# Self-attention rows of groups two to four: read turned from memory and normalised in place, instead of normalised and turned with TensorE

## The chip, the cores and the metric

The kernel runs on one core of one Trainium2 chip. The metric is the device time of one execution in microseconds (us). A core has five instruction streams that run side by side and wait for one another: TensorE (PE; its weight loads are listed apart as PEld), VectorE (DVE), ScalarE (ACT), GpSimd (POOL) and SyncE (SP, which issues most DMAs; POOL and ACT issue a few).

## The reference

The program is one decoder layer in float32 on 16 sequences of 128 rows, 1024 wide. Only its first stage matters here, single-head self-attention on the layer-normalised rows, per sequence of 128 rows, with a head of width 256:

```
x = x + attn(layernorm(x))
def layernorm(x): m = mean(x); v = var(x); return (x - m) / sqrt(v + 1e-5)
def attn(x):
    q, k, v = split(x @ Wqkv + bqkv, 3)            # Wqkv is 1024 x 768
    a = softmax(q @ k.T / sqrt(256))               # per sequence
    return (a @ v) @ Wo + bo                       # Wo is 256 x 1024
```

Cross-attention with a context and a feed-forward block with packed 4-bit weights follow. They make up the rest of the time and are not touched by the change.

## The kernel before

**Layout.** The 16 sequences are the residual tiles X[0] to X[15] (128 x 1024 each, 512 KB). Self-attention works in four groups t = 0..3 of four sequences. For each group it needs the normalised rows turned, a tile xnT of 128 x 8 x 512: eight chunks of 128 input columns, each over the 512 rows of the group.

**How xnT is made.** For a sequence b, `row_stats` (L130, L131) takes mean and variance on DVE; `row_rstd` (L135, L136) makes 1/sqrt(var + eps), an addition on DVE and a power on POOL; `normalise` (L139) writes xn on DVE; `turn_half` (L344) turns xn with four TensorE transposes into a PSUM tile `tr`, twice per sequence; and `turn` copies the two halves into xnT, one on DVE (L351) and one on ACT (L352). The first group has a version of its own, `first_rows`, with the normalisation on ACT (L152) and the copies on L63 and L368; its DVE instructions go through the wrapper InOrder (L63), which keeps them in program order among themselves.

**A group's work.** `query_key` (L397) multiplies the q and k columns of Wqkv with xnT, four blocks f of eight matmuls, copied out by ACT (L406). `value` (L412) makes v for each of the four sequences, with the bias added on DVE (L419). `weigh` (L427) makes the scores; DVE takes the row maximum (L435, L436), ACT the exponential (L440), DVE the reciprocal and the product `at` (L448, L449). `turn_weights` turns `at` (L457, copied by DVE, L459) and `attend` (L467) multiplies with v; ACT copies the result oT (L470). In the next group, between the blocks f, `give` (L295) multiplies oT with Wo and DVE adds it to X (L302). `add_bias` (L390) adds the output bias to X[b] on POOL, one 128 x 1024 addition per sequence; it needs the tile bo_sb. During group t the rows of group t+1 are normalised and turned.

**Beside it.** `early` is a generator that unpacks the feed-forward's 4-bit weights on DVE in the same stage: tiles pa and pc on L63, loads raw and sz on SP (L197, L198), stores on POOL (L214). Its steps are drawn between the blocks of groups 1 to 3.

**What orders the work.** Each engine runs its list of instructions strictly in its order. The lists are laid out when the program is built, by a scheduler that knows the dependences and estimates durations, not by the order of the source alone; the instructions of InOrder keep their own order, and others are put between them. DMAs of SP use eight completion counters in turn, so an SP DMA is not issued before the eighth one ahead of it has landed. The loads of the start are issued by SP in this order: X[0..3] (L329), five pieces of Wqkv (L332), the bias of v (L333), X[4..7] (L335), Wo (L336, 1 MB), bo_sb (L337, 512 KB), X[8..15] (L339), then the first raw and sz.

Of the kernel before, what the change touches and what calls it, by code (L numbers as in the profile page):

```python
# [11 lines left out]
F32 = mybir.dt.float32  # L12
I32 = mybir.dt.int32
AF = mybir.ActivationFunctionType
ALU = mybir.AluOpType
# [3 lines left out]
P = 128  # L19
B, S, C = 16, 128, 1024  # L20
# [5 lines left out]
EPS = 1e-5  # L26
CC = C // P
NB = C // P
TB = 512
BPT = TB // S  # L30
NT = B // BPT
JC = C // 2 // P
HB = B // 2
Q = 32
# [32 lines left out]
def decoder_layer(  # L67
    ctx: ExitStack,
    tc: tile.TileContext,
    x: bass.AP,  # L70
    cx: bass.AP,
    cxt: bass.AP,
    wqkv: bass.AP,
# [22 lines left out]
    nc = tc.nc  # L96
# [3 lines left out]
    small = ctx.enter_context(tc.tile_pool(name="small", bufs=4))  # L100
# [8 lines left out]
    X = []  # L109
# [12 lines left out]
    mv = stat.tile([P, B, 2], F32, name="mv")  # L122
    rstd = stat.tile([P, B], F32, name="rstd")
    mhalf = const.tile([P, BPT], F32, name="mhalf")
    nc.vector.memset(mhalf, -0.5)

    def row_stats(b, vector=nc.vector):
        st = small.tile([P, 2, 6], F32, name="bnst")
        for h in range(2):
            vector.bn_stats(st[:, h, :], X[b][:, ts(h, 512)])  # L130
        vector.bn_aggr(mv[:, b, :], st)  # L131

    def row_rstd(b0, n, vector=nc.vector):
        r = rstd[:, ds(b0, n)]
        vector.tensor_scalar(r, mv[:, ds(b0, n), 1], EPS, None, ALU.add)  # L135
        nc.gpsimd.tensor_tensor(r, r, mhalf[:, :n], ALU.pow)  # L136

    def normalise(dst, src, b):
        nc.vector.tensor_scalar(  # L139
            dst, src, mv[:, b, 0:1], rstd[:, b : b + 1], ALU.subtract, ALU.mult  # L140
        )
# [27 lines left out]
    dram = ctx.enter_context(tc.tile_pool(name="wdram", bufs=1, space=bass.MemoryType.DRAM))  # L169
# [145 lines left out]
    with (  # L315
# [17 lines left out]
        nc.sync.dma_start(bv_sb, bv.partition_broadcast(P).rearrange("p o f -> p (o f)"))  # L333
        for b in range(BPT, 2 * BPT):
            nc.sync.dma_start(X[b], x[b])  # L335
        nc.sync.dma_start(wo_sb, wo.rearrange("(dc p) c -> p dc c", p=P))  # L336
        nc.sync.dma_start(bo_sb, bo.partition_broadcast(P).rearrange("p o f -> p (o f)"))  # L337
        for b in range(2 * BPT, B):
# [2 lines left out]
        def turn_half(xn, xnT, b, h):  # L341
            tr = atr.tile([P, 4, P], F32, name="tr")
            for j in range(4):
                nc.tensor.transpose(tr[:, j, :], xn[:, ts(4 * h + j, P)], ident)  # L344
            return xnT[:, ts(h, 4), ts(b % BPT, S)], tr

        def turn(b, xnT):

            xn = a2.tile([P, C], F32, name="xn")
            normalise(xn, X[b], b)  # L350
            nc.vector.tensor_copy(*turn_half(xn, xnT, b, 0))  # L351
            nc.scalar.copy(*turn_half(xn, xnT, b, 1))  # L352

        def first_rows(xnT):

            vector = InOrder(tc, nc.vector)
            halves = {}

            def stats(b):
                row_stats(b, vector)  # L360
                row_rstd(b, 1, vector)

            def rows(b):
                xn = a2.tile([P, C], F32, name="xn")
                row_shift(b, vector)
                normalise_act(xn, X[b], b)
                halves[b] = turn_half(xn, xnT, b, 0)
                nc.scalar.copy(*turn_half(xn, xnT, b, 1))  # L368

            def copy(b):  # L370
                vector.tensor_copy(*halves[b])

            for fn, b in (
                (stats, 0),
                (stats, 1),
                (rows, 0),
                (rows, 1),
                (stats, 2),
                (copy, 0),
                (copy, 1),  # L380
                (stats, 3),
                (rows, 2),
                (rows, 3),
                (copy, 2),
                (copy, 3),
            ):
                fn(b)

        def add_bias(b):
            nc.gpsimd.tensor_tensor(X[b], X[b], bo_sb, ALU.add)  # L390

        def query_key(f, xnT, qkT, ps=None, tokens=slice(None)):

            if ps is None:
                ps = aps.tile([P, TB], F32, name="mm")
            for c in range(CC):
                nc.tensor.matmul(  # L397
                    ps[:, tokens],
                    wqkv_sb[:, f, c, :],
                    xnT[:, c, tokens],  # L400
                    start=(c == 0),
                    stop=(c == CC - 1),
                )
            if tokens == ts(0, TB // 2):
                return
            nc.scalar.activation(qkT[:, f, :], ps, AF.Identity, bias=bqk_sb[:, f : f + 1])  # L406

        def value(i, xnT, v):

            ps = aps.tile([P, DH], F32, name="mm")  # L410
            for c in range(CC):
                nc.tensor.matmul(  # L412
                    ps,
                    xnT[:, c, ts(i, S)],
                    wqkv_sb[:, 4:6, c, :],
                    start=(c == 0),
                    stop=(c == CC - 1),
                )
            nc.vector.tensor_tensor(v[:, i, :], ps, bv_sb, ALU.add)  # L419
# [34 lines left out]
        def turn_weights(at):  # L454
            tr = atr.tile([P, BPT, S], F32, name="tr")
            for i in range(BPT):
                nc.tensor.transpose(tr[:, i, :], at[:, i, :], ident)  # L457
            atT = a1.tile([P, BPT, S], F32, name="atT")
            nc.vector.tensor_copy(atT, tr)  # L459
            return atT  # L460

        def attend(atT, v):
            oT = ag.tile([P, 2, TB], F32, name="oT")
            for d in range(2):
                ps = aps.tile([P, BPT, S], F32, name="mm")
                for i in range(BPT):
                    nc.tensor.matmul(  # L467
                        ps[:, i, :], v[:, i, ts(d, P)], atT[:, i, :], start=True, stop=True
                    )
                nc.scalar.copy(oT[:, d, :], ps.rearrange("p i s -> p (i s)"))  # L470
            return oT

        def give(b, oT):
            for h in range(2):
                give_half(b, h, oT, [wo_sb[:, d] for d in range(2)], aps)

        xnTs = [a2.tile([P, CC, TB], F32, name="xnT")]
        first_rows(xnTs[0])  # L480
        oT = None
        for t in range(NT):
            xnT = xnTs.pop()
            more = t + 1 < NT
            if more:
                xnTs.append(a2.tile([P, CC, TB], F32, name="xnT"))
                for b in range((t + 1) * BPT, (t + 2) * BPT):
                    row_stats(b)
                row_rstd((t + 1) * BPT, BPT)
            qkT = a2.tile([P, 4, TB], F32, name="qkT")  # L490
            halves = {}
            if t == 0:

                for f in range(4):
                    halves[f] = aps.tile([P, TB], F32, name="mm")
                    query_key(f, xnT, qkT, halves[f], ts(0, TB // 2))
            for f in range(4):
                if t == 0:
                    query_key(f, xnT, qkT, halves[f], ts(1, TB // 2))
                else:  # L500
                    query_key(f, xnT, qkT)
                add_bias(t * BPT + f)
                if more:
                    if oT is not None:
                        give((t - 1) * BPT + f, oT)
                    turn((t + 1) * BPT + f, xnTs[0])
                if t > 0:
                    for _ in range(1 + f % 2):
                        next(early, None)
            v = a2.tile([P, BPT, DH], F32, name="v")  # L510
            value(0, xnT, v)
            at = weigh(qkT)
            if more:
                value(1, xnT, v)
                value(2, xnT, v)
                atT = turn_weights(at)
                value(3, xnT, v)
                if t == 0:
                    for _ in range(3):
                        next(early)  # L520
            else:

                for i in range(1, BPT):
                    give((t - 1) * BPT + i - 1, oT)
                    value(i, xnT, v)
                    next(early, None)
                atT = turn_weights(at)
                give(t * BPT - 1, oT)
            oT = attend(atT, v)
            for _ in range((3, 3, 3, 0)[t]):  # L530
                next(early, None)
# [106 lines left out]
    if True:  # L638
# [163 lines left out]
        def query_unit(b, pair, qs, wait):  # L802
# [43 lines left out]

            later(2, weigh)
            later(wait, turn)

        def turned(b):  # L850
# [800 lines left out]
    with ExitStack() as dst:  # L1651
# [126 lines left out]
        for n, oq in enumerate(DOWN):  # L1778
# [23 lines left out]
            for iq in INNER:  # L1802
# [13 lines left out]
                if iq == 1:  # L1816
                    t = kept["u"] = dt.tile(wide, F32, name="iu")
# [3 lines left out]
                elif iq == 6:  # L1821
                    t = kept["u"]
# [90 lines left out]
```

## Time and profile before

| what | value |
|---|---|
| device time, median of 3 runs | 2226.76 us (2226.05 to 2232.44) |
| span of the profiled execution | 2228.8 us |
| busy share of PE, DVE, ACT, POOL | 98%, 70%, 23%, 25% |
| self-attention stage | about 0 to 250 us |
| first matmul of `attend` in groups 0, 1, 2, 3 | 62.83, 125.85, 189.64, 248.78 us |
| first transposes on PE | 9.33 us |

The page gives the span of the profiled execution and no other time of it; the span lies inside the three runs. The page's first part says how long each engine was busy; the chain of waits follows the work that ended last back from the end, so that time on it is time of the kernel; the timeline lists instructions with their start and duration, and in brackets the idle time of the engine before them with what ended it. A matmul in float32 shows as two records. Spans of matmuls include a latency that overlaps with the next one, so the cost of a run of matmuls is read from start to start, or from the chain.

### The profile page before, as it was taken

To read this page: it belongs to the slowest core of one execution; us is meant where nothing else is said; L and a number is where in the kernel's file an instruction comes from. 1 tells how busy PE (TensorE), PEld (TensorE's weight loads), DVE (VectorE), ACT (ScalarE), POOL (GpSimd) and SP (SyncE) were. 2 spreads that over 40 slices of the span, in tenths; PEclk is the share of its full clock that TensorE was granted. 3 is DMA by queue.
4 is the path that set the end of the run, shared out by engine and by line. 5 is a ranking of instruction groups with operands and counts; after the bars stand their busy time and mean duration, and the time that the engine had idled before them with its cause. 6 is when DMAs were issued, how large, how long until landed. Compare 5 with 4: busy or idle time off the path is not lost.

```text
span 2228.8 us, 24449 instructions
## 1 busy us (share of the span) xinstructions
PE 2192.9 (98%) x8500; PEld 1547.7 (69%) x8500; DVE 1563.4 (70%) x2119; ACT 508.5 (23%) x684; POOL 564.2 (25%) x442
## 2 busy tenths in 40 slices
PE   8999999999999999999999899999999999999998
PEld 7556555555555544444888488888887788888887
DVE  7897577888887637667799778787786645544462
ACT  2111235665556531111121112122121000000000
POOL 5453133333333300001354134444442000000000
PEclk9999999999999999999999999999999999999999
DMA  6435447777796748899544835465555965334631
GB/s 253 158 130 185 142 144 242 226 228 231 234 290 190 241 137 263 254 292 303 183 135 137 231 113 164 158 199 164 167 195 180 346 200 179 101 124 138 219 118 40
DMA packets 268725, 425.27 MB, mean 191 GB/s; under 512 B 28784, under 2 KB 130544, under 8 KB 268464
## 3 DMA queue, kind: packets, MB, share of 16 engines
q1 hardware_dynamic: 239584, 368.54, 52.7%
q0 software_dynamic: 10704, 35.92, 4.4%
q10 hardware_dynamic: 18304, 19.14, 2.7%
q8 instruction: 70, 1.15, 0.2%
q14 instruction: 63, 0.52, 0.1%
HBM read 265.62 MB, written 157.35 MB: 190 GB/s over the span
## 4 chain that ended last, share of the span: by engine, by line
PE 88%; DVE 6%; DMA 3%; issue 2%; SPq 1%; ACT 0%; POOL 0%; DVEq 0%; ACTq 0%; POOLq 0%
PE q L63 24%; PE po L1792 21%; PE p L63 11%; PE kq L63 10%; PE mm L63 8%; PE kx L63 5%; PE mm L397 4%; PE p L1166 2%; DVE pa L63 2%; PE mm L412 2%; PE mm L295 1%; DVE ti L63 1%; DMA wd<-pc 1%; PE tr L344 1%; DVE C L63 1%
## 5 line engine op out<-in xcount | busy, mean ns | idle before, releaser
L63 PE MATMUL q<-ti,li 128*128 128x256 f32 x1176 | 271.6, 380 | 2.9 <-DVE ti L63 1.4
L63 PEld LDWEIGHTS q<-ti,li 128*128 128x128 f32 x1176 | 222.5, 190 | 37.0 <-POOL li L63 4.5
L63 POOL TENSOR_TENSOR li<-w 128x512 f32<-128x512 f32 x98 | 141.2, 1443 | 342.9 <-DMA wd<-pc 235.2
L63 PE MATMUL p<-b,w 128*128 128x512 f32 x432 | 194.1, 602 | 12.5 <-DVE h L63 12.0
L825 POOL TENSOR_TENSOR qe<-qe,qrec 128x1024 f32<-128x1024 f32 x64 | 148.1, 2314 | 180.1 <-DVE qrec L63 156.0
L63 ACT COPY k<-q 128x512 f32<-128x512 f32 x147 | 86.0, 585 | 468.8 <-PE q L63 467.6
L1792 PE MATMUL po<-wc,lc 128*128 128x256 f32 x840 | 183.4, 379 | 0.0
L1792 PEld LDWEIGHTS po<-wc,lc 128*128 128x128 f32 x840 | 159.6, 190 | 21.8
L63 PEld LDWEIGHTS p<-b,w 128*128 128x128 f32 x432 | 82.9, 193 | 118.0 <-issue 100.9
L63 PE MATMUL p<-T,w 128*128 128x512 f32 x304 | 134.7, 592 | 0.0
L1792 PE MATMUL po<-wq,lq 128*128 128x256 f32 x560 | 126.7, 379 | 0.3 <-issue 0.3
L63 PEld LDWEIGHTS mm<-qs,m_sb 128*128 128x128 f32 x512 | 97.3, 190 | 40.1 <-issue 29.4
L63 DVE STREAM_TRANSPOSE kt<-qe 128x1024 f32<-128x1024 f32 x64 | 79.4, 1240 | 64.5 <-POOL qe L825 58.1
L63 PE MATMUL kq<-wq_sb,xn 128*128 128x512 f32 x256 | 120.3, 593 | 1.6 <-ACT qe L813 1.6
L63 PE MATMUL kx<-ek,cxt 128*128 128x512 f32 x256 | 121.8, 598 | 0.0
L63 PE MATMUL mm<-qs,m_sb 128*128 128x256 f32 x512 | 120.8, 379 | 0.0
L63 PE MATMUL kq<-wk_sb,cx 128*128 128x512 f32 x256 | 120.1, 592 | 0.0
L1792 PEld LDWEIGHTS po<-wq,lq 128*128 128x128 f32 x560 | 106.0, 190 | 15.9 <-issue 1.1
L397 PE MATMUL mm<-xnT,wqkv_sb 128*128 128x512 f32 (+1 forms) x320 | 113.2, 510 | 0.0
L63 POOL TENSOR_TENSOR li<-w,li 128x512 f32<-128x512 f32 x49 | 66.3, 1352 | 183.7 <-PE q L63 172.6
L63 DVE TENSOR_TENSOR pa<-pa,sz 128x1024 f32<-128x1024 int32 x86 | 108.8, 1265 | 2.4
L63 PEld LDWEIGHTS p<-T,w 128*128 128x128 f32 x304 | 57.8, 190 | 72.7 <-issue 72.2
(193 smaller groups left out, 3759.9 us busy)
## 6 DMA issues: line engine op xcount, KB each, us to landing
w<-wu SPq DMA_DIRECT2D x140, 256.0 KB, 3.5
lq<-h SPq DMA_DIRECT2D x140, 256.0 KB, 4.4
w<-wg SPq DMA_DIRECT2D x138, 256.0 KB, 2.9
kd<-kt SPq DMA_DIRECT2D x64, 512.0 KB, 3.7
qs<-kd SPq DMA_DIRECT2D x256, 128.0 KB, 3.5
h<-hc SPq DMA_DIRECT2D x80, 256.0 KB, 2.9
wq<-wd SPq DMA_DIRECT2D x70, 256.0 KB, 5.2
h<-h SPq DMA_DIRECT2D x60, 256.0 KB, 2.1
```

Source lines behind the costliest of these rows:

```text
L63: return lambda *args, **kw: self._tc.keep_in_program_order(fn(*args, **kw))
L295: tensor.matmul(ps, oT[:, d, ts(b % BPT, S)], wo_d[d][:, ts(h, 512)], start=(d == 0), stop=(d == 1),)
L344: nc.tensor.transpose(tr[:, j, :], xn[:, ts(4 * h + j, P)], ident)
L397: nc.tensor.matmul(ps[:, tokens], wqkv_sb[:, f, c, :], xnT[:, c, tokens], start=(c == 0), stop=(c == CC - 1),)
L412: nc.tensor.matmul(ps, xnT[:, c, ts(i, S)], wqkv_sb[:, 4:6, c, :], start=(c == 0), stop=(c == CC - 1),)
L825: nc.gpsimd.tensor_tensor(qe, qe, rec.unsqueeze(2).to_broadcast(wide), ALU.mult)
L1166: tensor.matmul(ps, wt[:, j, :], T[q][:, :, j], start=(first == q and j == 0), stop=(q in (2, 3, 4) and j == JC - 1), skip_group_check=True,)
L1792: nc.tensor.matmul(bank[:, i, :], l[:, ts(i, S)], w,  start=(start and c == 0 and i % 2 == 0), stop=(stop and c == len(pairs) - 1), skip_g ...
```

## The change

For groups 1 to 3 the transposes on PE, the tile xn and the copies out of PSUM are gone. The host hands over a second copy of the input, `xt`, in the layout of xnT; `load_rows` loads it with two DMAs of 1 MB per group straight into the xnT tile. Now the rows lie along the free dimension, and the mean and the scale of a row have to be the same in all partitions. `spread_stats` makes them so: after the statistics, an addition on DVE, a power on POOL and a multiply on DVE put rstd and -mean*rstd of the group's four sequences into eight columns of a tile gst; DVE turns gst in 32 x 32 blocks; four DMAs of 8 x 32 elements write it into a DRAM tile; one DMA reads that back, spread over all partitions, as `both` (128 x 2 x 512, 512 KB). `normalise_part` then works on xnT in place on DVE, two chunks at a time: a product with the first half of `both` and a sum with the second, two tensor-tensor instructions of 128 x 1024, four times per group. The per-group `row_rstd` goes. The load of group 1 stands between X[4..7] and Wo among the loads of the start; those of groups 2 and 3 are issued when the xnT tile two groups back is free. `first_rows` is as before.

```diff
@@ loads of the start
         for b in range(BPT, 2 * BPT):
             nc.sync.dma_start(X[b], x[b])
+        xnTs = [a2.tile([P, CC, TB], F32, name="xnT") for _ in range(2)]
+        def load_rows(t):
+            for h in range(2):
+                nc.sync.dma_start(xnTs[-1][:, ts(h, CC // 2)], xt[t, :, ts(h, CC // 2)])
+        load_rows(1)
         nc.sync.dma_start(wo_sb, wo.rearrange("(dc p) c -> p dc c", p=P))
         nc.sync.dma_start(bo_sb, bo.partition_broadcast(P).rearrange("p o f -> p (o f)"))
@@ helpers
-        def turn(b, xnT):
-            xn = a2.tile([P, C], F32, name="xn")
-            normalise(xn, X[b], b)
-            nc.vector.tensor_copy(*turn_half(xn, xnT, b, 0))
-            nc.scalar.copy(*turn_half(xn, xnT, b, 1))
+        gst = aw.tile([P, Q], F32, name="gst")
+        nc.gpsimd.memset(gst, 0.0)
+        def spread_stats(t):
+            r, sh = (gst[:, ds(8 * t + 4 * n, BPT)] for n in range(2))
+            m = mv[:, ds(t * BPT, BPT)]
+            nc.vector.tensor_scalar(r, m[:, :, 1], EPS, None, ALU.add)
+            nc.gpsimd.tensor_tensor(r, r, mhalf, ALU.pow)
+            nc.vector.scalar_tensor_tensor(sh, m[:, :, 0], -1.0, r, ALU.mult, ALU.mult)
+            rows = small.tile([P, Q], F32, name="gst_rows", bufs=2)
+            nc.vector.transpose(rows, gst)
+            flat = dram.tile([8, 4, Q], F32, name="gst_flat", tag="gst_flat", bufs=2)
+            for q in range(4):
+                nc.sync.dma_start(flat[:, q], rows[ds(Q * q + 8 * t, 8)])
+            both = a2.tile([P, 2, TB], F32, name="both", tag="xn")
+            flat = flat.rearrange("(w i) q s -> w (i q s)", w=2)
+            nc.sync.dma_start(both, flat.partition_broadcast(P))
+            return both
+        def normalise_part(xnT, f, both):
+            part = xnT[:, ts(f, 2)]
+            for w, op in ((0, ALU.mult), (1, ALU.add)):
+                nc.vector.tensor_tensor(
+                    part, part, both[:, w].unsqueeze(1).to_broadcast([P, 2, TB]), op
+                )
@@ the loop over groups
-        xnTs = [a2.tile([P, CC, TB], F32, name="xnT")]
         first_rows(xnTs[0])
         oT = None
         for t in range(NT):
-            xnT = xnTs.pop()
+            xnT = xnTs.pop(0)
             more = t + 1 < NT
             if more:
-                xnTs.append(a2.tile([P, CC, TB], F32, name="xnT"))
+                if t > 0:
+                    xnTs.append(a2.tile([P, CC, TB], F32, name="xnT"))
+                    load_rows(t + 1)
                 for b in range((t + 1) * BPT, (t + 2) * BPT):
                     row_stats(b)
-                row_rstd((t + 1) * BPT, BPT)
+                both = spread_stats(t + 1)
...
                     if oT is not None:
                         give((t - 1) * BPT + f, oT)
-                    turn((t + 1) * BPT + f, xnTs[0])
+                    normalise_part(xnTs[0], f, both)
@@ host
+        "xt": a["x"].reshape(NT, TB, CC, P).transpose(0, 3, 2, 1),
```

More of the change, by code (lines that the diff above doesn't have):

```diff
@@ L70, in decoder_layer @@
     x: bass.AP,
+    xt: bass.AP,
     cx: bass.AP,
```

## The prediction

> **What bounds the kernel now.** I read the page's busy shares first, then the chain of waits, then the stage that the change touches, from the timelines of PE, DVE, POOL and SP between 0 and 250 us. From the page, the chain that ended last, by engine:
>
> ```profile
> PE 88%; DVE 6%; DMA 3%; issue 2%; SPq 1%; ACT 0%; POOL 0%; DVEq 0%; ACTq 0%; POOLq 0%
> ```
>
> TensorE sets the time. In the self-attention stage the list of waits has PE idle for 9.3 us at the start and 1.0 us after it (0.83 before the second group's `attend`, 0.2 before a transpose). Some pieces of the same chain, kept to this stage (start, length, what):
>
> ```profile
> 9.33 3.68 PE tr L344 x16
> ...
> 33.09 0.87 PE tr L344 x8
> ...
> 59.54 3.47 PE mm L412 x16
> 63.03 0.04 DVE v L419
> ...
> 139.19 0.87 PE tr L344 x8
> ```
>
> One sequence's eight transposes cost PE 0.87 us, 0.109 each, against twice that (0.23) for the very first ones. The chain leaves PE at 63.03 and comes back at 127.5: in the second group DVE is all but the bound. Busy time by stretch says the same (the columns are PE, PEld, DVE, ACT, POOL):
>
> ```profile
> 80.00:100.00 20.00, 20.00 (x60) 9.66 (x59) 19.90 (x29) 2.55 (x4) 13.24 (x14) 1.00 0.46 151
> 100.00:120.00 20.00, 20.00 (x86) 14.14 (x85) 19.90 (x38) 2.45 (x9) 7.56 (x12) 1.00 0.51 174
> ```
>
> DVE is busy for 19.9 us in 20 here, while PE never stops. So PE time removed is a gain only while DVE keeps pace.
>
> POOL's additions of the output bias, and the DVE products beside one of them:
>
> ```profile
> 26.47 17.78 POOL L390 TENSOR_TENSOR X<-X,bo_sb 128x1024 f32<-128x1024 f32 x7 [0.55 <-issue]
> 44.21 1.02 POOL L136 TENSOR_TENSOR rstd<-rstd,mhalf 128x4 f32<-128x4 f32 x1
> 45.20 2.36 POOL L390 TENSOR_TENSOR X<-X,bo_sb 128x1024 f32<-128x1024 f32 x1
> 85.62 3.21 POOL L390 TENSOR_TENSOR X<-X,bo_sb 128x1024 f32<-128x1024 f32 x1
> ```
> ```profile
> 79.09 1.20 DVE L63 TENSOR_TENSOR pa<-pa,sz 128x1024 f32<-128x1024 f32 x1
> ...
> 87.14 2.77 DVE L63 TENSOR_TENSOR pa<-pa,sz 128x1024 f32<-128x1024 f32 x1
> ```
>
> An addition takes 2.36 us alone and 3.2 beside a DVE product, which then takes 2.77 instead of 1.20. POOL begins at 26.47, as soon as bo_sb is there: SP issued it at 13.52 and it took 12.8 to land.
>
> **What is removed.** 96 transposes, 12 sequences at 0.87 us: 10.4 us of PE, all on the path: 3.5 in each of groups 0, 1 and 2. ACT's 12 copies were off it (ACT 23% busy). DVE loses 12 copies (0.68 us, 0.60 from start to start) and 12 normalisations (0.72 alone, up to 2.8 beside POOL).
>
> The Trainium skill's page "TensorE: Matmul & The Clock Gate", Part 4 on the PE-mode transpose, has one at about 275 ns in a kernel; this trace has 292 as a mean duration, but the eight start 0.109 us apart. By the page's figure the change would take away 26 us and win; the spacing decides, and the sum goes by 0.87.
>
> **What is added, and where it falls.** I read the lists of the changed kernel, built but not run. After self-attention they are the same on all engines, so what is lost or won by then stays. In the first group they are not. POOL (its rows 11 to 22) and DVE (rows 50 to 59):
>
> ```
> 11 L364 TensorTensor gst<-gst,mhalf 128x4            (power, group 1)
> 12-21 L420 TensorTensor X<-X,bo_sb 128x1024          (ten bias additions, X[0] to X[9])
> 22 L364 TensorTensor gst<-gst,mhalf 128x4            (power, group 2)
>
> 50 L363 TensorScalarPtr gst<-mv 128x4                (group 2)
> 51 L365 TensorScalarPtr gst<-mv,gst 128x4            [waits Pool]
> 52 L367 StreamTranspose gst_rows<-gst 128x32
> 53-58 L380 TensorTensor xnT<-xnT,both 128x1024, x8   (group 1)
> 59 L449 TensorTensor v<-mm,bv_sb 128x256             (group 0)
> 60 L465 TensorReduce nmax<-mm 128x4                  (group 0)
> ```
>
> So group 2's power stands behind ten bias additions, DVE waits for that power, and behind this wait stand all of group 1's normalisation and then group 0's own v and softmax, for which PE waits. Step by step:
>
> 1. The 2 MB of xt stand ahead of Wo and bo_sb in SP's queue. Between 18.68 and 22.53 SP issues a load every 1.28 us, each as the eighth before it lands, so 512 KB land in 1.28 us and 2 MB in 5.1. bo_sb landed at 13.52 + 12.8 = 26.3; now at 31.4.
> 2. Ten additions at 2.36: 31.5 + 23.6 = 55.1. The power, 1.02: 56.1. Two small DVE instructions (0.14 for the row `shift`; the 32-wide transpose between 0.06 and 1.24, from 1.24 for 128x1024; I take 0.2): 56.5.
> 3. Eight tensor-tensor instructions of 128x1024. In place with a spread operand they are like pa<-pa,sz: 1.20 each, 9.6. POOL goes on with X[10] and X[11] beside them; beside two earlier additions DVE lost 1.56 us in one product and 2.0 in two (4.50 for 2.48), so two cost 0 to 4, I take 3.6. DVE reaches v at 69.7 (66.1 to 72).
> 4. From v to `at` ready: before, v at 51.01 and `at` at 56.09 with a wait for PE inside; without it v, maximum and scale 1.3, ACT and the rest 2.55: 3.95 in all. Then PE's transposes of `at` (0.44) and the last `value` (3.46).
> 5. PE has nothing after its third `value`. Its first rows are late as well (DVE's list has the statistics of X[4] and X[5], which land at 18.7 and 20.0, ahead of the shifts for X[2] and X[3]), by some 5 us; it would get to the wait near 48, and it waits until about 74. That hides the 5 us, and all of group 0's saved 3.5.
> 6. After the idle start of the run PE needed 4.5 us (9.33 to about 13.9) until its spacing fell to the full rate, and lost half of it. The granted clock reads 1.00 there all the same. After 26 us of idle I take the same 2.2; the other end is 0.
>
> `attend` of group 0 then starts at 69.7 + 3.95 + 3.9 + 2.2 = 79.8, against 62.83: **17.0 late**.
>
> The same page of the Trainium skill ("TensorE: Matmul & The Clock Gate", Part 1, on the clock gate) lets PE fall to half rate after an idle window of about 3.4 us and back after as long a busy one. By that step 6 would be 1.7 instead of 2.2. It speaks against any change that trades PE work for a PE wait.
>
> **Groups 1 and 2.** From there to the second `attend` DVE took 64.0 us (63.37 to 127.38). It loses four copies (2.4), two normalisations (1.4), the wait for POOL and two more (2.8), statistics that move behind (1.5) and two bias additions beside it, now earlier (1.56 + 2.0); it gains eight products of 1.2 (9.5): 61.8, and up to 3 more for X[12] and X[13]. PE needs 64.7 - 1.0 - 3.5 = 60.2. I take 62.5, **2.2 back** (0 to 4.5). Behind DVE's two new waits (power, then `both`) stand the bias sums that free PSUM; group 1's `both` is hidden by the wait above: its last gst write is issued when X[11] lands (36.6), queued behind X[15] (37.7 + 5.1 = 42.8), and two DMAs at 4 to 5 us (2 KB of bqk took 4.0, raw 3.5) end by 52.
>
> In group 2 PE has 62.1 - 3.5 = 58.7. DVE had 50.3 busy, with 6 us lost beside POOL; it gains 9.6, loses 4.3 (copies, two normalisations), takes over 1.5 and drops about 3 of the loss: 54. Group 3's power stands behind the additions to X[12..15], and four writes and `both` follow: some 4 us of DVE wait. That just fits; I take 1 us of stall, **2.5 back** (0 to 3.5). SP's loads of xt wait for PE to leave the old xnT and hold up raw and sz behind them; each 1 MB lands in about 4.6 (2 + 2.6), before DVE asks for it 5.7 us later.
>
> **Sum.** 17.0 - 2.2 - 2.5 = 12.3. The profiled span of 2228.8 becomes 2241.1; it lies 2.0 above the median of the runs, so the time is 2226.8 + 12.3 = **2239**. With every term at its low end (v at 66.1, no slow restart: 11.1; 4.5 and 3.5 back) it is +3.1, 2230. At the high end (v at 72: 19.2; nothing back) it is +19.2, 2246; a gst chain longer than bounded may add two.
>
> **Rivals.**
> - *The hold is weak* (2233, chance 0.17): no loss beside POOL and no slow restart, as in the low end, or one of them. For it: DVE's products beside the addition at 85.62 lost nothing until 87.1. Against: the rows above.
> - *Faster* (2222, chance 0.08): group 1's normalisation starts when `both` lands, not when POOL's tenth addition is done. At 47 it would end at 56.6, `attend` would start at 64.5, 1.7 late, and 2.2 to 8 come back: -0.5 to -6.3. It decides if normalising begins before about 50. Against: DVE's list is in order and row 51 stands ahead of 53; for it, only that additions may take less time with DVE quiet, and 2.345 is the shortest of ten.
> - *DVE bound to the end* (2247, chance 0.17): additions beside it and the two chains of small DMAs eat all that groups 1 and 2 give back. For it: 19.9 in 20.
> - That the transposes stay is no case: the list of PE has only the first group's and those of `at`.
>
> **How the numbers follow.** The forecast (2234 to 2245) has 0.56, the rest as above, 0.02 for anything else. A measurement here tells 0.3%, 6.7 us, from no change: below 2220 is faster, above 2233.5 slower. Of the faster rival about half passes the bound: 0.04. Same: the rest of it and two thirds of the weak hold, 0.16. Slower: 0.80. The range 2230 to 2248 leaves out the faster rival and a tail above.
>
> **What would show it.** PE idle for 20 to 28 us before the first transposes of `at`; POOL's first bias addition near 31.5 and its second power of four near 55; DVE idle before that, then eight products in 10 to 14 us; `attend` of group 0 near 80; the last `attend` 9 to 15 later than 248.78. It is wrong if v of group 0 comes before 62, or if the third `attend` trails by under 5.

## The result, and the profile after

The changed kernel takes **2244.43 us** (median of 4 runs, 2243.06 to 2246.63); the kernel before took 2229.0 in the same setting (median of 4, 2226.05 to 2232.44). The ratio is 1.007, with a 95% interval of 1.0054 to 1.0087: slower by 15 us. The profiled execution has a span of 2241.4 (2228.8 before) and a time of 2243.25. The forecast was 2239 in a range of 2230 to 2248.

Where does it go? First the changed kernel's chain of waits by engine, as the page has it:

```profile
PE 84%; DVE 8%; DMA 4%; issue 2%; POOL 2%; ACT 1%; SPq 0%; DVEq 0%; ACTq 0%; POOLq 0%
```

PE's share of the chain fell from 88% to 84%; DVE, POOL and DMA took it over. In the list of PE's waits (what waits and for what: us in total, times, longest) two rows grew and one shrank; before they had 9.3, 0.2 and 12.0:

```profile
PE tr L353 <- ACT xn L153: 15.3, 2, 9.7
PE tr L487 <- DVE at L479: 15.1, 2, 10.1
PE p L63 <- DVE h L63: 8.7, 2, 6.5
```

The first has the known 9.7 at the start and a new 5.6; the second is PE's wait for the softmax weights, in groups 0 and 2; the third lies far behind the stage. The longer pieces of the chain itself, in order of time (start, length, what), show who made the wait of group 0:

```profile
36.56 18.55 POOL X L420 x8
55.10 0.99 POOL gst L364
56.12 4.62 DVE gst L365
60.90 9.13 DVE xnT L380 x8
70.36 0.61 DVE nmax L465
71.25 1.51 ACT at L470 x8
73.00 0.70 DVE at L479
73.84 1.09 PE tr L487 x4
74.93 5.35 PE mm L442 x16
```

These are bias additions on POOL, the power behind them, DVE's small sum (gst) that waits for the power, eight products, and only then group 0's own softmax. No PE work stands in it between 36 and 73. POOL's timeline has the additions (start, length, line, operation, in brackets the idle time before it); beside it DVE's row for the small sum:

```profile
31.93 23.17 POOL L420 TENSOR_TENSOR X<-X,bo_sb 128x1024 f32<-128x1024 f32 x10 [3.51 <-DMA bo_sb<-in_bo]
55.03 1.05 POOL L364 TENSOR_TENSOR gst<-gst,mhalf 128x4 f32<-128x4 f32 x1
56.02 4.69 POOL L420 TENSOR_TENSOR X<-X,bo_sb 128x1024 f32<-128x1024 f32 x2
```
```profile
56.12 4.61 DVE L365 SCALAR_TENSOR_TENSOR gst<-mv,gst 128x4 f32<-128x4 f32 x1 [17.13 <-POOL gst L364]
```

Read the two together. The sum over 128 x 4 elements takes 0.16 us elsewhere. Here it starts 0.10 after POOL has begun the additions to X[10] and X[11] and ends at 60.73, 0.02 after they do. By these times it did not run slowly; it was held until both additions were done. How the hold falls differs from kernel to kernel: in stats_pinned and warm, two of the experiments below, where POOL's list is the same here, the sum took 2.30 beside the first of the two additions, and the eight products 11.13 and 11.16 (9.13 here) beside the second. Together that is 4.1 to 4.2 us lost instead of 4.5. PE's side of it, and below it the same three rows of the kernel before:

```profile
73.84 1.09 PE L487 MATMUL tr<-ident,at 128*128 128x128 f32 x4 [10.07 <-DVE at L479]
74.72 5.54 PE L442 MATMUL mm<-wqkv_sb,xnT 128*128 128x256 f32 x16
80.10 2.06 PE L497 MATMUL mm<-atT,v 128*128 128x128 f32 x16
```
```profile
58.94 0.60 PE L457 MATMUL tr<-ident,at 128*128 128x128 f32 x4
59.37 3.62 PE L412 MATMUL mm<-wqkv_sb,xnT 128*128 128x256 f32 x16
62.83 2.06 PE L467 MATMUL mm<-atT,v 128*128 128x128 f32 x16
```

After a wait of 10.07 the four transposes take 1.09 instead of 0.60 and the `value` 5.54 instead of 3.62, and `attend` of group 0 starts at 80.10 instead of 62.83. The granted clock reads 0.50 from 73.84 to 78.00. This is called the slow restart below. The start of `attend` in each group is the best ruler for this stage; the interval of a group is the time from the start before to its own. For all kernels, with these starts as PE's timeline has them (those of the kernel before differ by 0.17 from the small table in groups 2 and 3) and the ratio to the kernel before on the same chip:

| kernel | attend 0 | 1 | 2 | 3 | median us (runs) | ratio, 95% interval |
|---|---|---|---|---|---|---|
| before | 62.83 | 125.85 | 189.47 | 248.61 | 2229.0 (4) | |
| changed | 80.10 | 139.35 | 206.16 | 265.30 | 2244.43 (4) | 1.0054 to 1.0087 |
| adds_moved | 68.39 | 127.65 | 194.77 | 253.91 | 2231.72 (10) | 1.0007 to 1.0026 |
| stats_pinned | 80.09 | 139.34 | 205.97 | 265.12 | 2244.5 (4) | 1.0047 to 1.0081 |
| no_norm | 60.07 | 125.82 | 184.96 | 244.10 | 2223.82 (10) | 0.9964 to 0.9983 |
| warm | 76.97 | 136.22 | 202.58 | 261.72 | 2243.55 (4) | 1.004 to 1.0074 |
| adds_late | 68.74 | 128.11 | 187.42 | 252.79 | 2235.71 (6) | 1.0021 to 1.0044 |
| late_stats | 71.41 | 130.67 | 189.95 | 255.32 | 2237.8 (6) | 1.0031 to 1.0056 |
| late_stats_bo | 74.83 | 134.08 | 193.16 | 258.51 | 2240.59 (5) | 1.004 to 1.0066 |
| before_load | 69.39 | 136.07 | 198.72 | 257.85 | 2237.7 (7) | 1.0021 to 1.0045 |
| before_load_pinned | 65.59 | 129.57 | 193.19 | 252.33 | 2232.53 (11) | 1.0013 to 1.0031 |
| dve_adds | 67.41 | 130.39 | 189.58 | 248.72 | 2226.51 (12) | 0.998 to 0.9997 |
| before_dve | 62.21 | 125.10 | 188.72 | 247.86 | 2227.97 (11) | 0.9988 to 1.0006 |
| dve_adds_act | 66.57 | 128.90 | 189.71 | 248.85 | 2225.45 (11) | 0.9983 to 1.0001 |

The last `attend` of the changed kernel is 16.7 late, the span only 12.6, while the medians of the runs differ by 15.4. In these two profiled executions 4.1 us come back later, mostly in the third row of the waits above (12.0 to 8.7). That row varies by 1 to 3 us between kernels with the same work there (8.7 to 12.0 in the runs below), so totals a few us apart say less than the `attend` columns.

### The profile page after: what moved, and what is told of

It is laid out like the page before. It is cut to its first block, busy times and chain, and to the rows that moved or that the text cites. A ratio compares the mean times of both kernels' runs of the same rounds, so it can differ in the third digit from the quotient of the medians.

```text
span 2241.4 us, 24271 instructions
## 1 busy us (share of the span) xinstructions
PE 2188.3 (98%) x8404; PEld 1542.8 (69%) x8404; DVE 1559.8 (70%) x2125; ACT 501.0 (22%) x672; POOL 558.2 (25%) x443
## 4 chain that ended last, share of the span: by engine, by line
PE 84%; DVE 8%; DMA 4%; issue 2%; POOL 2%; ACT 1%; SPq 0%; DVEq 0%; ACTq 0%; POOLq 0%
PE q L63 23%; PE po L1823 21%; PE p L63 11%; PE kq L63 10%; PE mm L63 8%; PE kx L63 5%; DVE pa L63 2%; PE p L1197 2%; DMA X<-in_x 1%; DVE ti L63 1%; POOL X L420 1%; PE mm L427 1%; PE mm L442 1%; DVE xnT L380 1%; DMA szd<-in_dsz 1%
```

## The experiments

**The theory:** the time is lost on POOL and DVE: bias additions on POOL stand ahead of the power and hold DVE, PE waits, and loses more through a slow restart. **The rivals:** the late first rows; the loads of `xt` and the late bo_sb; the normalisation's own DVE time, which would leave nothing to gain wherever the additions stand.

### adds_moved: the additions out of group 1's way

```diff
-                add_bias(t * BPT + f)
+            for b in (range(0, 8), (), range(8, 12), range(12, 16))[t]:
+                add_bias(b)
```

The loop stands behind spread_stats(t + 1), with add_bias on POOL through InOrder.

> The bias additions are placed by hand on POOL: X[0] to X[7] ahead of group 2's power, X[8..11] in group 2, X[12..15] in group 3. Theory (the hold on POOL and DVE makes the loss): the second power moves from 55.0 to about 50.6 and no addition runs beside the small DVE sum behind it (4.6 us becomes 0.2), so the eight products run from 52 to 61, the first attend starts near 69.4 instead of 80.1, and the stall of group 2 shrinks because X[12..15] are no longer added at its start: 10 to 16 us less than the changed kernel. Rival (DVE simply has too much work, the hold is a symptom): the first attend comes earlier, but groups 1 and 2 stretch and at most 5 us are won.

Measured: 2231.72, 12.7 us under the changed kernel. The power of group 2 ran at 50.12 instead of 55.03, nothing stood beside DVE's small sum (0.16), PE waited 1.71 and restarted at full rate: 4.9 + 4.5 + 2.4 make the 11.7 by which `attend` 0 came earlier. The rows of adds_moved:

```profile
50.12 1.04 POOL L364 TENSOR_TENSOR gst<-gst,mhalf 128x4 f32<-128x4 f32 x1
51.20 0.16 DVE L365 SCALAR_TENSOR_TENSOR gst<-mv,gst 128x4 f32<-128x4 f32 x1 [10.23 <-POOL gst L364]
64.47 0.63 PE L487 MATMUL tr<-ident,at 128*128 128x128 f32 x4 [1.71 <-DVE at L479]
```

That part is settled. The power still stands behind eight additions, and `attend` 0 is still 5.6 later than before; no run puts the power ahead of all additions while they stay on POOL. The expected shrinking of group 2's stall failed: PE waited 5.90 there (4.98 in the changed kernel). The reason is in the timelines of adds_moved, DVE and POOL in group 2:

```profile
136.98 2.31 DVE L365 SCALAR_TENSOR_TENSOR gst<-mv,gst 128x4 f32<-128x4 f32 x1 [0.94 <-POOL gst L364]
139.21 2.91 DVE L63 TENSOR_TENSOR pc<-pa 128x512 f32<-128x512 f32 x1
142.03 0.20 DVE L367 STREAM_TRANSPOSE gst_rows<-gst 128x32 f32<-128x32 f32 x1
142.16 5.18 DVE L63 TENSOR_TENSOR pc<-pc,pa 128x512 f32<-128x512 f32 x1
```
```profile
136.92 4.64 POOL L63 TENSOR_TENSOR X<-X,bo_sb 128x1024 f32<-128x1024 f32 x2
141.51 0.60 POOL L215 DMA_DIRECT2D wg<-pa  x1
142.14 4.65 POOL L63 TENSOR_TENSOR X<-X,bo_sb 128x1024 f32<-128x1024 f32 x2
```

The additions to X[8..11], which the edit put into group 2, now do there what others did in group 0: sums that take 0.16, 0.68 and 0.68 took 2.31, 2.91 and 5.18, 8.9 us more.

### stats_pinned: the first rows on time

```diff
-                    row_stats(b)
+                    row_stats(b, InOrder(tc, nc.vector) if t == 0 else nc.vector)
```

> The statistics of X[4..7] are kept behind the first rows' DVE instructions. Theory: PE's wait of 5.6 us ahead of the transposes of X[2] and X[3] goes, PE then waits longer before the transposes of the weights, the first attend stays within 1 us of 80.1 and the time within 2 us of the changed kernel. Rival (the late start is paid for once more): 5 to 7 us less.

Measured: 2244.5, and `attend` 0 at 80.09 (80.10). PE's wait for the third xn is 1.29 instead of 5.64, and its wait for the weights 17.99 instead of 10.07. The late first rows cost nothing here; that rival is out.

### no_norm: without statistics and products

```diff
-                for b in range((t + 1) * BPT, (t + 2) * BPT):
-                    row_stats(b)
-                both = spread_stats(t + 1)
...
-                    normalise_part(xnTs[0], f, both)
+                    pass
```

> Leaves out, for groups 1 to 3, the statistics, the spreading and the products, so q, k and v of these rows come from x as it was loaded. Theory (96 transposes are worth 10.4 us of PE, the loads of xt cost nothing by themselves): all DVE waits of PE in self-attention go and the time is 10 to 12 us below the kernel before. Rival (the loads, or something beside the transposes, cost as well): less than 6 us below it.

Measured: 2223.82, 5.2 us faster than before, not 10 to 12. Group 0 gains 2.8, but group 1 has a PE wait of 4.03 for `at` and a slow restart (1.09, 5.59). POOL's sixteen additions follow one another there from 32.52 to 72.30, and four DVE instructions beside them, between 60.95 and 72.58, take 2.0 to 2.2 us more each than alone, 8.4 together; that is more than the wait. So half of the 10.4 us of transposes does not come back here even when the normalisation is free, and POOL's additions are the likely cause; no run takes them out of no_norm.

### warm: PE kept busy through its wait

```diff
+                if t == 0:
+                    spare = atr.tile([P, 4, P], F32, name="tr")
+                    for n in range(22):
+                        tc.keep_in_program_order(
+                            nc.tensor.matmul(spare[:, 0:2].rearrange("p a b -> p (a b)"),
+                                xnT[:, n % CC, ts(0, S)], wqkv_sb[:, 4:6, n % CC, :], start=True, stop=True))
                 atT = turn_weights(at)
```

> 22 products of 128x256 into a spare PSUM tile (9.5 us, results unused) fill PE's wait in group 0. Theory (an idle PE starts again at half rate): from the transposes of the weights to the first attend it takes 3.9 to 4.2 us instead of 6.3, the first attend starts 2.2 us earlier and the time is about 2 us less. Rival (the slow stretch comes from the engines around it): no change in either.

Measured: with PE busy until 0.32 before the transposes these took 0.63, the `value` 3.62, and `attend` 0 started 3.92 after the transposes instead of 6.26. The restart is worth 2.3 us, and idle time makes it. In the stage it is won: the last `attend` starts 3.6 earlier. The total moved by 0.9 (2243.55), inside the spread; group 2's wait (4.93, with its slow restart) was still there.

### adds_late and late_stats: no addition in groups 1 and 2

Against adds_moved:

```diff
-            for b in (range(0, 8), (), range(8, 12), range(12, 16))[t]:
+            for b in (range(0, 8), (), (), range(8, 16))[t]:
```

> As adds_moved, but the bias additions to X[8] to X[15] all stand in group 3, where DVE has no products; none is left in groups 1 and 2. Theory A: in adds_moved group 2 stalled because four additions at 136.92 to 146.79 on POOL held DVE (the 128x4 sum took 2.31 instead of 0.16, two 128x512 sums 2.91 and 5.18 instead of 0.68: 8.9 us together), so the PE wait of 5.90 for the weights of group 2 and the slow restart behind it go: interval of group 2 from 67.1 to about 59.2, last attend at 246 to 248 (253.91 in adds_moved), total 2224 to 2227. Rival B: DVE is simply full in group 2, products included, and the stall of at least 4 us stays wherever the additions are: last attend 251 to 254, total 2230 to 2233. Rival C: the eight additions in group 3 hold DVE there, and the stall moves to group 3: intervals 59, then 65 or more.

Measured: the stall of group 2 is gone (no wait, interval 59.31), as theory A had it; rival B is out. DVE still waits 2.94 for `both` in that group (2.67 in the changed kernel), so that wait alone does not stall PE. Rival C is right too: in group 3 the interval grew to 65.4. DVE's and POOL's rows of adds_late there:

```profile
199.24 14.35 DVE L63 TENSOR_TENSOR pc<-pc,pa 128x512 f32<-128x512 f32 x1
213.51 0.68 DVE L63 TENSOR_TENSOR pc<-pa 128x512 f32<-128x512 f32 x1
```
```profile
199.19 13.84 POOL L63 TENSOR_TENSOR X<-X,bo_sb 128x1024 f32<-128x1024 f32 x6
```

One sum of 128 x 512 elements, 0.68 us of work, stood for 14.35 us: as long as six additions that follow one another without a gap. It is the clearest line of this study, and late_stats and late_stats_bo repeat it: the same sum takes 14.33 in both. (Not every sum waits for a whole run: just before it, sums of 1.22 and 0.68 took 3.25 and 2.73, one addition each.) The last `attend` (252.79) and the total missed theory A. The total was 2235.71, 4 above adds_moved, though the stage ended 1.1 earlier; a new wait of 2.6 follows just behind the stage (for rstd on DVE). The rest is open, and the trace cannot settle it: the profiled execution, 2232.46, was the shortest of the six.

late_stats is adds_late with the edit of stats_pinned as well.

> adds_late with the row statistics of X[4] to X[7] pinned behind the first rows, so that PE's wait of 5.6 us for the third xn goes. Theory: attend of group 0 is set by the chain bo_sb, eight additions, power, DVE's sum, products (all on POOL and DVE), so PE only waits later for as much: attend 0 at 68.4 within 0.5, total as adds_late within 2 us. Rival: PE's lateness is the bound by now (its wait before the weights is only 1.71 us in adds_moved), and attend 0 comes 1.5 to 5 us earlier, and the total with it.

Measured: 71.41, 2.7 *later* than adds_late, and 2237.8. The rival's gain did not come, but the theory's mark (68.4) was missed too: the additions began 0.6 later (bo_sb landed later), and with PE's wait grown from 0.72 to 8.64 the slow restart came back (1.08, 5.28), 2.1 us.

### late_stats_bo: the load of `xt` behind bo_sb

```diff
-        load_rows(1)
         nc.sync.dma_start(wo_sb, ...)
         nc.sync.dma_start(bo_sb, ...)
+        load_rows(1)
```

> late_stats with the load of xt for group 1 issued behind bo_sb instead of ahead of it. Theory: bo_sb lands 5 us earlier (about 26.4), and the additions, the power, the products and v follow: additions 26.5 to 45, products from 47 to 56, attend 0 at 63 to 64 (68.4 before), since xt, landing at about 31, is needed only at 47; total 4 to 5 us under late_stats. Rival: PE sets attend 0 by now, or xt's landing does, and it stays at 67 or later.

Measured: 74.83, later by 3.4, and 2240.59. The experiment did not test what it was meant to: with the loads moved, the lists put a statistic of X[8], which DVE waited for until 33.70, ahead of the end of group 1's statistics. Power and additions, which stand behind them, began at 36.26. What an earlier bo_sb is worth stays open (it landed at 26.7 here, but the power stood ahead of the additions).

### before_load and before_load_pinned: the loads alone

```diff
+        xnTs = [a2.tile([P, CC, TB], F32, name="xnT") for _ in range(2)]
...
+        load_rows(1)
```

These are the kernel before with the loads (those of groups 2 and 3 as well); the transposes overwrite what they bring. before_load_pinned has the edit of stats_pinned too.

> The kernel before with the loads of xt alone: they go into the tiles that the transposes write later, so that the loads' place in the queue, their traffic and the lateness of bo_sb are in, and no statistics, products or removal. It takes the kernel's second xnT tile from the start, too. Theory: the loads cost nothing by themselves; bo_sb lands near 31.5 and moves the additions by 5 us, which the kernel before hardly feels, because its products wait for no power queued behind additions: attend 0 at 62.8 to 65, total 2229 to 2232. Rival: the traffic or the late bo_sb is the larger part of the slowdown: attend 0 at 68 or later and total 2234 to 2241.

> before_load with the row statistics of X[4] to X[7] pinned behind the first rows. In before_load attend 0 came 6.56 us later, and TensorE waited 4.69 us for the third xn, because DVE stood at the statistics of X[4]. Theory: that order, and not the traffic or the late bo_sb, is what the loads alone cost in group 0: attend 0 at 62.8 to 64 again, and of the 9.2 us at the end of the stage 5 to 7 go; total 2230 to 2233. Rival: the late bo_sb or the traffic costs it: attend 0 stays at 67 or later, total 2235 to 2239.

Measured: 2237.7 for the first, so my theory was wrong and the rival's numbers held: `attend` 0 at 69.39. But the traffic and the late bo_sb are not the whole cause: with the statistics pinned, 65.59 and 2232.53 (the total as that theory had it, `attend` 0 between its mark and the rival's). Of the 9.2 us at the end of the stage 5.5 come from the order in which the lists were laid out (DVE stands at the statistics of X[4], PE waits 4.69), and 3.7 remain for the loads: in before_load_pinned POOL begins its additions at 32.70, and PE waits 1.88 for a copy on DVE beside them and 1.14 for `at` in group 1. So the changed kernel's loads are not free, though in the changed kernel itself the first part is hidden (stats_pinned).

### dve_adds and before_dve: no addition on POOL

```diff
-            nc.gpsimd.tensor_tensor(X[b], X[b], bo_sb, ALU.add)
+            InOrder(tc, nc.vector).tensor_tensor(X[b], X[b], bo_sb, ALU.add)
```

In dve_adds X[0..3] are added behind the products of group 0, X[4..7] behind its turned weights, X[8..15] in group 3, and the statistics are pinned; in before_dve X[0..7] in group 0, X[8..15] in group 3.

> The changed kernel with no bias addition on POOL: DVE does them, X[0] to X[3] behind the products of group 0, X[4] to X[7] behind the copy of the turned weights of group 0, X[8] to X[15] in group 3; the statistics of X[4] to X[7] stand behind the first rows. Theory: the time was lost because a DVE sum of two tensors cannot run while POOL's additions run (one 128x512 sum took 14.35 us beside six of them in adds_late), so sixteen sums of about 1.20 on DVE cost less than sixteen of 2.36 on POOL that hold it: power of group 2 at about 40, products 40 to 49, four additions to 54, v at 54.3, attend 0 at 60.5 to 62, then three intervals of 59.2, last attend at 238 to 242 (265.30 in the changed kernel, 248.61 before), total 2218 to 2224, faster than before by 0.2 to 0.5%. Rival: DVE is full in groups 1 and 2 (59.9 us busy of 60 in adds_moved), the eight products of each group do not fit beside the decoding of the weights, and two intervals are 63 or longer: last attend at 247 or later, total 2228 or more.

> The kernel before with its bias additions on DVE instead of POOL: X[0] to X[7] in group 0, X[8] to X[15] in group 3. It shows what the move of the additions is worth without the change. Theory: the kernel before is bound by TensorE in this stage (its waits there are 1 us in all), so little comes back, only the few us that TensorE lost in groups 1 and 2 beside the ideal 60: attend 0 at 62.8 to 65, last attend at 246 to 250, total 2227 to 2231. Rival: POOL's additions held this kernel as well, and it gains 3 us or more: total 2226 or less.

Measured: dve_adds 2226.51, 18 us under the changed kernel and 2.3 under the kernel before (ratio 0.998 to 0.9997). The total lies between the theory's and the rival's, and the last `attend` (248.72) where the rival had it. The 18 us belong to the whole edit: the pinned statistics changed nothing in the changed kernel, but by the medians 5.2 us in before_load. Two intervals are 59.2 as expected, so in groups 2 and 3 DVE keeps pace, and in group 2 the eight products do fit beside the decoding; there the rival fails. Group 0 missed its mark by 5.4 us (67.41). Group 1 needed 63.0; of the 3.8 more, 1.7 are `attend` 0 at the slow restart (3.78 instead of 2.06) and 1.6 two waits of PE for DVE. DVE's rows of dve_adds show what was late next:

```profile
47.81 9.17 DVE L380 TENSOR_TENSOR xnT<-xnT,both 128x1024 f32<-128x1024 f32 x8 [6.58 <-DMA both<-gst_flat]
56.90 4.62 DVE L63 TENSOR_TENSOR X<-X,bo_sb 128x1024 f32<-128x1024 f32 x4
```

The products wait for `both`, issued by SP at 43.86 because its writes stand behind the loads of X. Four additions take 4.62, 1.16 each. before_dve is at 2227.97, no different from before, as expected: the old kernel did not suffer from POOL. Between the two kernels with additions on DVE the difference of 1.5 us cannot be told from none, and in the stage dve_adds is not ahead: its last `attend` is 0.9 later.

### dve_adds_act: the read-back from another queue

```diff
+            queue = nc.scalar if t == 1 else nc.sync
-                nc.sync.dma_start(flat[:, q], rows[ds(Q * q + 8 * t, 8)])
+                queue.dma_start(flat[:, q], rows[ds(Q * q + 8 * t, 8)])
-            nc.sync.dma_start(both, flat.partition_broadcast(P))
+            queue.dma_start(both, flat.partition_broadcast(P))
```

> dve_adds with group 1's statistics written and read back from the ACT queue instead of SP's. In dve_adds DVE stood 6.58 us at 41.2 for `both`, whose write waited in SP's queue behind seven loads of X (gst_rows ready at about 26.4, the write issued at 33.84, `both` at 43.86). Theory: on ACT's queue, idle from 18.2 to 33.8, the write goes out at about 27, `both` lands before 37, the products run from 39.4 to 48.5 behind the statistics of X[8] to X[11], v at about 54, attend 0 at 60.5 to 62.5 instead of 67.41, and the two waits of 5.86 and 0.78 go with the slow restart (attend 3.78 instead of 2.06): last attend at 240 to 243 (248.72), total 2219 to 2223. Rival: the read-back is late because the 16 DMA engines are busy with the loads (the share of the first 40 us is 80 to 99%), not because of the queue's order; `both` lands at 42 or later and 3 us or less come back: total 2224 or more.

Measured: 2225.45 (ratio 0.9983 to 1.0001), `attend` 0 at 66.57, stage end as in dve_adds. The rival's total came true, but not by its cause alone. The writes went out at 26.72 to 31.5 and `both` was issued at 35.46, 8.4 earlier than from SP's queue; it reached DVE at 41.71, 6.1 earlier, since it took 6.25 to arrive instead of 3.95. So the queue's order was a large part of the delay, and the slower transfers among the loads another. Of these 6.1 us PE got little. Group 2's sum now stands between the additions and v, so the transposes began only 4.5 earlier (61.06 for 65.54) and PE still waits 4.31. And the lists now put the last `value` behind the transposes, at the slow restart (4.79); in dve_adds PE had done it before its wait. That leaves 0.8 us at `attend` 0.

## Why the prediction was right, and where it was not

The sum (+12.3) and its direction held: the spans differ by 12.6, the medians by 15.4. For group 0 this is the mechanism that was forecast. That the total comes so near is partly luck: the last `attend` was 16.7 late, not 12.3, because group 2 lost time instead of giving it back, and in the profiled execution 4.1 came back behind the stage, where the prediction had said that nothing would change. By its steps:

1. **bo_sb later, additions from 31.5:** 31.93. Right.
2. **Ten additions, power at 55.1:** 55.03. Right.
3. **v at 69.7:** 69.94. Two additions held DVE, as said, but not where I had put it: 3.6 us of loss were to fall into the eight products (10 to 14 us in all); they ran at full speed (9.13), and the small sum ahead of them was held for 4.61. That the sizes agree is partly luck, since 3.6 was a choice between 0 and 4. The step took from the rows of before that POOL slows DVE, not that it stops it. The Trainium skill has this rule: its page "SBUF — State Buffer", section "Who interferes with whom", says that a DVE instruction with two inputs in SBUF contends with a GpSimd instruction that reads SBUF, and its summary that the one issued later is blocked until the first finishes. The runs agree, and go further: some sums here waited for one addition (2.31 in adds_moved), but one for two in a row (4.61) and one for six (14.35).
4. **`at` 3.95 after v:** the transposes start 3.90 after it. Right, though the two parts given for it (1.3 and 2.55) make 3.85.
5. **PE waits 20 to 28 us:** wrong; it waited 10.07. PE reached the wait at 63.77, not 48. I had counted the matmuls of group 0's q and k from the list of instructions and taken a timeline's duration per record for each, but a matmul shows as two records, so I halved their 25 us. The kernel before would have given the warning: its PE reaches this place at 58.94, and less 3.5 for the transposes and plus 5 for the late rows that makes 60.4. `attend` did not depend on it, since DVE was later still, so the sum was spared. The late first rows were a wait of 5.64 (5 said), with a slow restart behind it (the granted clock reads 0.50 from 22.00 to 24.60), and hidden, as said: stats_pinned.
6. **Slow restart 2.2:** 2.4 here, and 2.3 in warm, where it was taken away. The granted clock shows it in this place (0.50 from 73.84 to 78.00). In these runs the waits of 4.0 to 18.0 before the transposes of `at` all cost a restart of 1.6 to 2.6 us, those up to 1.71 none, and two in between, of 2.05 and 2.17, cost 1.5 and 1.7. The Trainium skill's "TensorE: Matmul & The Clock Gate", Part 1, gives a window of about 3.4 us; by that these last two waits alone would not have been long enough.

`attend` 0 was 17.3 late (17.0 said). **Group 1** gave back 3.8 instead of 2.2 (interval 59.25, before 63.02): no addition fell into it before 136, so DVE was full and still in time. **Group 2** was the term of the sum that failed: 2.5 back was forecast, with 0 as the worst case, and 3.2 were lost (interval 66.81, before 63.62). Additions to X[12..15] begin at 136.17, and DVE's pairs of TENSOR_SCALAR that take 0.75 took 3.71 and 3.01 beside them; then the chain of power, writes and `both` made DVE wait 2.67 at 162.35. PE paid with 4.98 and a second slow restart:

```profile
136.17 7.53 POOL L420 TENSOR_TENSOR X<-X,bo_sb 128x1024 f32<-128x1024 f32 x3
146.47 3.25 POOL L420 TENSOR_TENSOR X<-X,bo_sb 128x1024 f32<-128x1024 f32 x1 [2.77 <-DVE bnst L131]
```
```profile
140.28 3.71 DVE L63 TENSOR_SCALAR pa<-raw 128x512 int32<-128x512 int32 x2
147.44 3.01 DVE L63 TENSOR_SCALAR pa<-raw 128x512 int32<-128x512 int32 x2
162.35 3.50 DVE L380 TENSOR_TENSOR xnT<-xnT,both 128x1024 f32<-128x1024 f32 x3 [2.67 <-DMA both<-gst_flat]
```
```profile
199.68 1.09 PE L487 MATMUL tr<-ident,at 128*128 128x128 f32 x4 [4.98 <-DVE at L479]
```

adds_late shows that without additions there the interval is 59.3, though its wait for `both` is as long. The forecast had left about 3 us of loss beside POOL in this group and taken 1 us of stall from it all; the two pairs alone lost 5.2, and the restart (2.6) was not in it. The last `attend` was thus 16.7 late (9 to 15 said). In the stage, the rival *DVE bound to the end* came nearer than my forecast: groups 1 and 2 together gave back 0.6 of the 4.7 that I had put down. *Faster* did not come: DVE's list had the power's wait ahead of the products, and the power ran at 55.03.

What the change is worth by itself: dve_adds against before_dve gives 1.5 us by the medians, which cannot be told from none, and no_norm, where the normalisation costs nothing, 5.2 with the additions on POOL. Where the 10.4 us on PE go in dve_adds can be read from the table, against before_dve: group 2's interval is 4.4 shorter, group 1's the same, and `attend` 0 comes 5.2 later. Group 0 loses more than group 2 wins, since PE waits there for DVE, which had waited 6.58 for `both` and then had eight products and four additions ahead of v.

## What to carry to other kernels

Before work is moved to DVE in a form with two inputs from SBUF, look at what GpSimd does in the same stretch: a run of its additions can stop such an instruction until the run ends, and all that stands behind it on DVE's list stops too, while instructions with one SBUF input lost at most one addition in these runs, and copies from PSUM nothing. Read the order of the lists, not the source: a power of 1 us behind ten additions of 2.36 was the largest term here. When PE's work is removed, name what PE will wait for next, and add about 2 us for each wait longer than 2.

## What the runs showed of the hardware that was not expected

- A DVE sum of two SBUF tensors often does not get between GpSimd additions that follow one another: 0.68 us of work took 14.35 beside six (adds_late; 14.33 in late_stats and late_stats_bo), 0.16 took 4.61 beside two; others got in after one (2.31, 3.25), and the sum that took 4.61 in the changed kernel took 2.30 in stats_pinned and warm. What decides is open. Normalisations with one SBUF input were held for one addition at most: in the kernel before 128 x 1024 took 2.33 us on average beside the additions, 0.81 in before_dve without them. 128 x 1024 additions cost 1.16 each on DVE and 2.36 on POOL.
- The slow restart hardly depends on the length of the wait: 2.4 us after 10.07, 2.6 after 4.98, 2.4 after 4.03, 1.9 after 17.99 (stats_pinned), 1.8 after 12.30, none after 1.71. After 2.17 (before_load) the transposes took 0.70 but the `value` 5.28, and after 2.05 (dve_adds_act, group 1, with 0.78 more behind the transposes) `attend` took 3.57 instead of 2.06.
- A 512 KB read-back over all partitions reached DVE 3.95 us after its issue where most loads had ended (dve_adds), and 6.25 later among them (dve_adds_act).
